# A message-passing layer on one core: layernorm by 625 nodes on 125 rows, with h's bfloat16 terms taken from it

## The chip, the core and the metric

The kernel runs on one core of a Trainium2 chip. A core has five engines that work side by side, each through its own queue of instructions in program order: TensorE (PE in the profile, its weight loads PEld), VectorE (DVE), ScalarE (ACT), GpSimd (POOL) and SyncE (SP). They wait for each other by semaphores. Transfers between the chip's memory and the on-chip memory (128 partitions, called rows here) are issued by SP, ACT or POOL and carried out by 16 DMA engines. TensorE writes into PSUM, a small memory that VectorE and ScalarE read.

The metric is device time in microseconds (us) of the whole kernel, the median of several runs; lower is better.

## The reference: what is computed

There are 6250 nodes of 64 features and 206250 edges, sorted by their destination. `x` is normalised and clipped, one message is formed for each edge from its source's row and the edge's own features, messages are summed by destination, and two small products with a residual end it:

```python
h = jnp.maximum(_layernorm(x, axis=-1), 0.0)
msg = jax.nn.relu(h[src] + edge_attr)
agg = jax.ops.segment_sum(msg, dst, num_segments=x.shape[0])
z = h + agg
out = x + jax.nn.relu(z @ W1 + b1) @ W2 + b2
```

## The kernel before

**Groups.** Edges go in 201 groups of 1024 (8 columns of 128 edges) and a short last one, numbered 0 to 201. For each group `load` (L171) brings the edge features `ea` by SP and the sources' rows `xg`, one column at a time, by an indirect transfer on POOL (`gather`, L161). The buffers of `ea` and `xg` are nine deep (`LOOK`); group g + 9 is loaded into group g's buffer once `messages(g)` (L465) has read it. `messages` adds the two and clips the sum, `one_hot` (L442) marks each edge's destination inside a window of 48 nodes, `window_sum` (L478) multiplies the two on TensorE, and `sum_into_z` (L438) adds the window to `z`, which holds h with its features on the rows.

**The first four groups** are gathered from `x` while h isn't yet there, and `norm_edges` (L420) normalises their rows on the spot. All later ones are gathered from `h_rows`, a copy of h in the chip's memory.

**Sets.** From group 4 on, two groups make a set of 16 columns, and six of them (four of an even group, two of an odd one) don't go by POOL: TensorE picks those rows from h on the chip. The nodes lie in ten parts of 625 (`SB`), each of five blocks of 125 (`BB`, `BN`). `hp` holds h as three bfloat16 terms that add up to it, a node to a row. For each set k, these stages run one or two sets ahead of their use: `hold` and `mask` (L335, L342) put an edge's place within its part and its node's number into one-hot form; `source` (L351) multiplies them into a list of wanted nodes, which makes a trip through the chip's memory to be spread over all rows (`source_row`, `sources`); `find` (L370) compares that list with the node numbers of each row; `slots_of` (L386) multiplies the result with `hp`; `back` (L378) compares `spots`, which each edge's place was written to earlier, with place numbers; and `pick` (L411) multiplies to bring each edge its row. The order of all this is written out by hand in `half` (L532), with no scheduler behind it.

**The beginning.** `x_sb` holds x with four nodes to a row in blocks of 512 nodes, twelve blocks and a rest of 106. `ln_head` (L187: mean, subtraction, squares) and `ln_rows` (L199: variance, root, h) run over three blocks at a time, then over the rest; `ln_rows` also writes `h_rows`, and `ln_turn` (L217) transposes h into `z`. Between these, `ranks` (L249), a generator with a `yield` after each of its steps, works out each set edge's part, its node inside the part, and its place; four of its steps run beside the layernorm, eight inside `norm_edges` of groups 0 to 3. ScalarE's queue starts with ten loads (L101 to L122): the rest of `src`, all of `dst`, the tails of both, and the four weights. After the layernorm `slot` is made from `dst` (L598 to L612). Groups 0 to 3 then run (L616). After them, `h_rows` is read back with 125 nodes to a row's block and split into the three terms (L626 to L636), edges' spots are worked out, transposed and written (L637 to L648), the first set's stages run alone (L651 to L655), and the main loop begins.

**The end.** `hidden`, `result` and `store` (L488 to L516) finish blocks of 512 nodes as soon as all edges of a block are summed, one stage at a time through `blocks_behind` (L520); `hidden` also loads the block's old rows `xb`. The last lines do so for block 11 and for the rest of 106 nodes.

The lines of the main order:

```python
        for g in range(2 * K0):
            half(g, sets=False)
        for _ in steps:
            pass
    ln_stack.close()
...
    spot(K0)
    hold(K0)
    mask(K0)
    for g in range(2 * K0):
        half(g, groups=False)
    for g in range(2 * K0, NG + 1):
        half(g)
```

Of the kernel before, what the change touches and what calls it, by code (L numbers as in the profile page):

```python
# [20 lines left out]
P = 128  # L21
# [6 lines left out]
TJ = 3  # L28
# [9 lines left out]
XC = 3  # L38
# [23 lines left out]
def kernel(  # L62
# [29 lines left out]
    x_sb = lnp.tile([P, NB + 1, R, D], F32, name="x_sb", bufs=1)  # L92
    for c in range(0, NB, XC):
        nc.sync.dma_start(
            out=x_sb[:, c:c + XC].rearrange("p b r d -> p b (r d)"),
            in_=x[c * P * R:(c + XC) * P * R, :].rearrange("(b p r) d -> p b (r d)", p=P, r=R),
        )
    nc.sync.dma_start(out=x_sb[:TN, NB, 0, :], in_=x[NB * P * R:, :])


    nc.scalar.dma_start(out=src_sb[:, RAW * G:C], in_=src_main[:, RAW * G:])  # L101
    nc.scalar.dma_start(out=dst_sb[:, :C], in_=dst_main)
# [7 lines left out]
    for t_sb, tail in ((src_sb, src_tail), (dst_sb, dst_tail)):  # L110
        flat = tail.rearrange("p j -> (p j)")
        nc.scalar.dma_start(out=t_sb[:, CP - CT:CP - 1], in_=flat[:TJ * P].rearrange("(p j) -> p j", j=TJ))
        nc.scalar.dma_start(out=t_sb[:, CP - 1:], in_=flat[TE - P:].rearrange("(p j) -> p j", j=1))
# [5 lines left out]
    nc.scalar.dma_start(out=w1_sb, in_=w1)  # L119
    nc.scalar.dma_start(out=w2_sb, in_=w2)  # L120
    nc.scalar.dma_start(out=b1_sb, in_=b1.rearrange("(d o) -> d o", o=1))
    nc.scalar.dma_start(out=b2_sb, in_=b2.rearrange("(o d) -> o d", o=1).to_broadcast([P, D]))  # L122
# [21 lines left out]
    hp = const.tile([P, KB, 3, D], BF16, name="hp")  # L144
    nc.vector.memset(hp[:, KB - 1], 0.0)
# [41 lines left out]
    def ln_head(c):  # L187
        xv, p, n = ((x_sb[:, c:c + XC].rearrange("p b r d -> p (b r) d"), P, XC * R) if c < NB
                    else (x_sb[:TN, NB, 0:1, :], TN, 1))
        s = lnp.tile([P, XC * R], F32, name="ln_s")  # L190
        nc.vector.tensor_reduce(s[:p, :n], xv, AX.X, ALU.add)
        nc.vector.tensor_scalar_mul(s[:p, :n], s[:p, :n], 1.0 / D)
        xc = lnp.tile([P, XC * R, D], F32, name="ln_xc")
        nc.vector.tensor_tensor(xc[:p, :n], xv, s[:p, :n].unsqueeze(2).to_broadcast([p, n, D]), ALU.subtract)
        sq = lnp.tile([P, XC * R, D], F32, name="ln_sq")
        nc.scalar.activation(sq[:p, :n], xc[:p, :n], AF.Square)
        return c, xc, sq, p, n

    def ln_rows(c, xc, sq, p, n):  # L199
        v = lnp.tile([P, XC * R], F32, name="ln_v")  # L200
        nc.vector.tensor_reduce(v[:p, :n], sq[:p, :n], AX.X, ALU.add)
        nc.scalar.activation(v[:p, :n], v[:p, :n], AF.Sqrt, bias=eps_sb[:p], scale=1.0 / D)
        nc.vector.reciprocal(v[:p, :n], v[:p, :n])
        h = lnp.tile([P, XC * R, D], F32, name="ln_h", bufs=3)
        nc.vector.scalar_tensor_tensor(h[:p, :n], xc[:p, :n], 0.0,
                                       v[:p, :n].unsqueeze(2).to_broadcast([p, n, D]),
                                       op0=ALU.max, op1=ALU.mult)
        if c < NB:
            nc.sync.dma_start(
                out=h_rows[c * P * R:(c + XC) * P * R, :].rearrange("(b p r) d -> p b (r d)", p=P, r=R),  # L210
                in_=h.rearrange("p (b r) d -> p b (r d)", r=R),
            )
        else:
            nc.sync.dma_start(out=h_rows[NB * P * R:, :], in_=h[:TN, 0, :])
        return c, h

    def ln_turn(c, h):  # L217
        for b in range(XC if c < NB else 1):
            pt = psum.tile([D, R, P], F32, name="rows", bufs=2)
            n0 = (c + b) * P * R  # L220
            if c < NB:
                for r in range(R):
                    nc.tensor.transpose(pt[:, r, :], h[:, b * R + r, :], ident)
                nc.scalar.copy(z[:, n0:n0 + P * R].rearrange("d (p r) -> d r p", r=R), pt)
            else:
                nc.tensor.transpose(pt[:, 0, :TN], h[:TN, 0, :], ident[:TN, :TN])
                nc.scalar.copy(z[:, n0:N], pt[:, 0, :TN])
# [5 lines left out]
    nc.gpsimd.iota(nodes_of, pattern=[[P, BB]], base=1, channel_multiplier=1, allow_small_or_imprecise_dtypes=True)  # L233
# [4 lines left out]
    fits = const.tile([P, KS, T], F32, name="fits")  # L238
# [10 lines left out]
    def ranks(pool):  # L249
# [11 lines left out]
        block = pool.tile([P, KS, T], F32, name="block")  # L261
        whole(block, src_f, BN)
        nc.vector.scalar_tensor_tensor(src_f, block, float(P - BN), src_f, op0=ALU.mult, op1=ALU.add)
# [20 lines left out]
        nc.vector.scalar_tensor_tensor(place, pt, float(-P), where, op0=ALU.mult, op1=ALU.add)  # L284
        nc.vector.tensor_scalar(fits, place, float(P), None, op0=ALU.is_lt)
        nc.vector.scalar_tensor_tensor(place, place, 1.0, fits, op0=ALU.add, op1=ALU.mult)

# [98 lines left out]
    def slots_of(k, m, n):  # L386

        ps = psum.tile([P, 2, 3 * D], F32, name="rows", bufs=2)
        for i in range(n):
            for b in range(BB):  # L390
                nc.tensor.matmul(ps[:, i], found[k][:BN, b, m + i, :],  # L391
                                 hp[:BN, (m + i) * BB + b].rearrange("p t d -> p (t d)"),
                                 start=(b == 0), stop=(b == BB - 1))
# [25 lines left out]

    def norm_edges(xg):  # L420
# [6 lines left out]
        next(steps, None)  # L427
# [3 lines left out]
        next(steps, None)  # L431
# [55 lines left out]

    def hidden(c):  # L488
# [4 lines left out]
        xb = work.tile([P, R, D], F32, name="xb")  # L493
        nc.sync.dma_start(out=xb[:p, :r].rearrange("p r d -> p (r d)"),
                          in_=x[n0:n0 + p * r, :].rearrange("(p r) d -> p (r d)", r=r))
# [36 lines left out]
    def half(g, groups=True, sets=True):  # L532
# [4 lines left out]
        if groups:  # L537
            enter(g + AHEAD)
# [9 lines left out]
        if groups:  # L548
            if g >= LAG:
                sum_into_z(g - LAG)  # L550
                blocks_behind(g - LAG)
            messages(g)
        if now and not even:
            slots_of(k + 1, 8, 2)
        if groups:
            take(g + 1)
# [5 lines left out]
        if groups and g >= 1:  # L562
            window_sum(g - 1)
# [15 lines left out]
        if groups:  # L579
            one_hot(g)  # L580
# [4 lines left out]
    with tc.tile_pool(name="rank", bufs=1) as rank:  # L585
        steps = ranks(rank)
        for c in range(0, NB + 1, XC):
            heads.append(ln_head(c))
# [7 lines left out]
        ln_turn(*rows[-1])  # L596

# [18 lines left out]
        for g in range(2 * K0):  # L616
            half(g, sets=False)
        for _ in steps:
            pass
    ln_stack.close()  # L620
    nc.vector.tensor_tensor(of_sets(slot, True), of_sets(slot, True), fits[:, :, :EVEN], ALU.mult)
    nc.vector.tensor_tensor(of_sets(slot, False), of_sets(slot, False), fits[:, :, EVEN:], ALU.mult)

    with tc.tile_pool(name="nodes", bufs=2) as nodes:

        for k, n in ((0, KB // 2), (KB // 2, KB - 1 - KB // 2), (KB - 1, 1)):  # L626
            p = min(BN, N - k * BN)
            h = nodes.tile([P, KB // 2, D], F32, name="h_nodes")
            if p == BN:
                nc.sync.dma_start(out=h[:BN, :n], in_=h_rows[k * BN:(k + n) * BN, :].rearrange("(k p) d -> p k d", p=BN))  # L630
            else:
                nc.sync.dma_start(out=h[:p, 0, :], in_=h_rows[k * BN:, :])
            nc.scalar.copy(hp[:p, k:k + n, 0, :], h[:p, :n])
            nc.vector.tensor_tensor(h[:p, :n], h[:p, :n], hp[:p, k:k + n, 0, :], ALU.subtract)
            nc.scalar.copy(hp[:p, k:k + n, 1, :], h[:p, :n])
            nc.vector.tensor_tensor(hp[:p, k:k + n, 2, :], h[:p, :n], hp[:p, k:k + n, 1, :], ALU.subtract)  # L636
        spot_f = nodes.tile([P, KS, T], F32, name="spot_f", bufs=1)  # L637
        nc.vector.scalar_tensor_tensor(spot_f, part, float(P), place, op0=ALU.mult, op1=ALU.add)
        spot_i = nodes.tile([P, KS * T], I16, name="spot_i", bufs=1)
        nc.vector.scalar_tensor_tensor(spot_i, spot_f.rearrange("p k t -> p (k t)"), float(BIAS - 1),  # L640
                                       fits.rearrange("p k t -> p (k t)"), op0=ALU.add, op1=ALU.mult)
        for c in range(0, KS * T, P):
            n = min(P, KS * T - c)
            turned = psum.tile([P, P], BF16, name="rows", bufs=2)
            nc.tensor.transpose(turned[:n], spot_i[:, c:c + n].bitcast(BF16), ident_b)
            sp = nodes.tile([P, P], BF16, name="sp")
            nc.scalar.copy(sp[:n], turned[:n])
            nc.sync.dma_start(out=spot_rows[c:c + n, :], in_=sp[:n])  # L648
    hot = ctx.enter_context(tc.tile_pool(name="hot", bufs=2))

    spot(K0)  # L651
    hold(K0)
    mask(K0)
    for g in range(2 * K0):
        half(g, groups=False)  # L655
# [83 lines left out]
```

## Time and profile before

| what | value |
|---|---|
| median of 3 runs | 1381.69 us (1381.45 to 1382.79) |
| the profiled execution | 1382.11 us, of it 1380.3 us in the span |
| busy, share of the span | PE 1251.2 (91%), PEld 1172.7 (85%), DVE 1194.2 (87%), ACT 510.0 (37%), POOL 1016.6 (74%) |
| chain that ended last | PE 50%, POOL 15%, DMA 12%, DVE 10%, issue 10%, ACT 2% |
| first gather from h_rows, last one | 51.96 us, 1362.37 us |
| last output transfer issued | 1375.91 us |

How to read it: the profile is one execution, from whose records the time of each instruction is known. A line of the costliest groups or of the timeline gives engine, source line, operation, output and inputs, shape, and in brackets how long the engine had stood before it and what ended that. "issue" stands for a wait that nothing in the records explains. DMA-issuing instructions are shown with a q (SPq, ACTq). A share of busy time is a mean over stages with different limits, so what holds the end has to be read stage by stage.

### The profile page before, as it was taken

The page shows a single profiled execution, that of the slowest core. Times are in us where ns is not written, and L with a number is a line of the kernel's source. Part 1 is how long each engine was busy: PE and PEld are TensorE (multiplying, and loading weights), DVE is VectorE, ACT ScalarE, POOL GpSimd, SP SyncE. Part 2 cuts the span into 40 slices and gives each one's busy share as a digit, 9 for nine tenths or more (in the row PEclk, how much of TensorE's full clock was granted, in tenths as well). Part 3 has the DMA queues.
Part 4 walks back from the last instruction along what each step waited for, and adds up shares of the span by engine and source line. Part 5 has one row for each costly group of instructions (what it writes and reads, how often), then busy time and mean ns, then how long its engine had stood idle before and what let it go on. Part 6 is the DMA issues. An engine that isn't in the chain of part 4 may idle for free.

```text
span 1380.3 us, 37812 instructions
## 1 busy us (share of the span) xinstructions
PE 1251.2 (91%) x15010; PEld 1172.7 (85%) x15010; DVE 1194.2 (87%) x2872; ACT 510.0 (37%) x1365; POOL 1016.6 (74%) x1029
## 2 busy tenths in 40 slices
PE   1623899999999999999999999999999999999997
PEld 0413799999999999999999998999998998988996
DVE  6765989889899899899899899899899898888984
ACT  2321334333433334334344333443334333433432
POOL 7671767777777777777777777777777777777773
PEclk9766999999999999999999999999999999999999
DMA  5332434444444444444444444444444344443431
GB/s 169 92 71 55 117 85 120 108 106 118 124 105 113 117 119 123 112 109 115 120 118 123 103 115 115 123 112 100 122 118 123 105 117 111 123 102 108 121 88 26
DMA packets 107888, 150.78 MB, mean 109 GB/s; under 512 B 33817, under 2 KB 52761, under 8 KB 107705
## 3 DMA queue, kind: packets, MB, share of 16 engines
q1 hardware_dynamic: 73881, 113.18, 28.2%
q0 software_dynamic: 32576, 33.42, 12.6%
q8 instruction: 119, 1.95, 0.6%
q10 hardware_dynamic: 1248, 1.70, 0.4%
q14 instruction: 64, 0.52, 0.1%
HBM read 144.60 MB, written 3.61 MB: 107 GB/s over the span
## 4 chain that ended last, share of the span: by engine, by line
PE 50%; POOL 15%; DMA 12%; DVE 10%; issue 10%; ACT 2%; DVEq 0%; SPq 0%; ACTq 0%; POOLq 0%
PE pick L417 23%; PE rows L391 16%; POOL xg L163 15%; PE agg L484 8%; DMA xg<-h_rows,src_sb 6%; DVE backs L383 3%; DMA ea<-in_edge_attr_dram 2%; DVE full L472 2%; PE rows L356 2%; DMA sources<-source_row 2%; DVE found L375 1%; DMA source_row<-source 1%; PE rows L505 1%; ACT picked L399 1%; DVE full L470 1%
## 5 line engine op out<-in xcount | busy, mean ns | idle before, releaser
L163 POOL DMA_INDIRECT xg<-h_rows,src_sb x986 | 982.1, 996 | 334.1 <-issue 258.6
L417 PE MATMUL pick<-picked,backs 128*128 128x192 bf16 x5940 | 524.0, 246 | 22.2 <-ACT pick L408 19.5
L417 PEld LDWEIGHTS <-backs 128*128 128x128 bf16 x5940 | 495.3, 98 | 26.7 <-issue 20.1
L391 PE MATMUL rows<-hp,found 125*128 125x192 bf16 x4950 | 465.2, 248 | 7.0 <-DVE found L375 6.1
L391 PEld LDWEIGHTS <-found 125*128 125x128 bf16 x4950 | 409.5, 98 | 18.7 <-DVE found L375 7.8
L383 DVE TENSOR_SCALAR backs<-spots,ids 128x768 bf16<-128x768 int16 x990 | 339.5, 415 | 0.0
L399 ACT CAST picked<-rows 128x384 bf16<-128x384 f32 x495 | 236.3, 477 | 277.4 <-PE rows L391 273.3
L375 DVE TENSOR_SCALAR found<-sources,nodes_of 125x1280 bf16<-125x1280 int16 x495 | 251.3, 572 | 36.7 <-DMA sources<-source_row 36.2
L472 DVE TENSOR_REDUCE full<-pick 128x128 f32<-128x512 f32 x297 | 207.7, 699 | 72.0 <-PE pick L417 41.4
L484 PEld LDWEIGHTS agg<-oh,msg 128*64 128x64 f32 x3224 | 205.0, 139 | 32.9 <-issue 17.9
L484 PE MATMUL agg<-oh,msg 128*64 128x48 f32 x3224 | 230.2, 225 | 0.6 <-ACT msg L475 0.6
L358 ACT CAST source<-rows 10x128 int16<-10x128 f32 x99 | 25.2, 254 | 464.2 <-PE rows L356 459.5
L475 ACT ACTIVATE msg<-full 128x512 f32<-128x512 f32 x202 | 119.5, 591 | 33.2 <-DVE full L472 20.3
L470 DVE TENSOR_TENSOR full<-full,xg 128x256 f32<-128x256 f32 (+1 forms) x202 | 98.7, 489 | 19.8 <-DMA xg<-h_rows,src_sb 15.4
L446 DVE TENSOR_TENSOR oh<-slot,wslots 128x384 f32<-128x384 int16 x202 | 109.6, 542 | 0.0
L338 DVE TENSOR_TENSOR holds<-place,wslots 128x768 f16<-128x768 f32 x99 | 93.2, 941 | 6.2 <-DMA spot_rows<-sp 6.2
L462 ACT COPY full<-ea 128x256 f32<-128x256 f32 (+1 forms) x202 | 87.0, 431 | 0.0
L408 ACT COPY pick<-ea 128x128 f32<-128x128 f32 x297 | 72.8, 275 | 0.0
L356 PE MATMUL rows<-holds,mask 128*10 128x128 f16 x594 | 50.1, 221 | 4.8 <-DVE mask L348 4.8
L356 PEld LDWEIGHTS <-mask 128*10 128x10 f16 x594 | 31.8, 88 | 22.1 <-issue 20.2
L440 DVE TENSOR_TENSOR z<-z,agg 64x48 f32 x202 | 38.3, 189 | 5.6 <-issue 2.9
L163 POOL DMA_INDIRECT xg<-in_x_dram,src_sb x32 | 32.7, 1021 | 11.2 <-issue 9.4
(105 smaller groups left out, 282.3 us busy)
## 6 DMA issues: line engine op xcount, KB each, us to landing
ea<-in_edge_attr_dram SPq DMA_DIRECT2D x201, 256.0 KB
sources<-source_row SPq DMA_DIRECT2D x99, 320.0 KB
spots<-spot_rows SPq DMA_DIRECT2D x99, 192.0 KB
xg<-h_rows,src_sb POOLq DMA_INDIRECT x986
source_row<-source SPq DMA_DIRECT2D x99, 2.5 KB
x_sb<-in_x_dram SPq DMA_DIRECT2D x4, 384.0 KB
h_rows<-ln_h SPq DMA_DIRECT2D x4, 384.0 KB
xb<-in_x_dram SPq DMA_DIRECT2D x12, 128.0 KB
```

Source lines behind the costliest of these rows:

```text
L163: nc.gpsimd.indirect_dma_start(out=xg[:, j, :], out_offset=None, in_=rows[:, :], in_offset=bass.IndirectOffsetOnAxis(ap=idx[:, j:j + 1], a ...
L356: nc.tensor.matmul(ps, mk[:, t, :], oh[:, t, :], start=(t == 0), stop=(t == T - 1))
L375: nc.vector.tensor_scalar(found[k][:BN, b].rearrange("p m s -> p (m s)"), row[:BN], nodes_of[:BN, b:b + 1], None, op0=ALU.is_equal)
L383: nc.vector.tensor_scalar(backs[k][:, m].rearrange("p t s -> p (t s)"), row, ids[:, m:m + 1], None, op0=ALU.is_equal)
L391: nc.tensor.matmul(ps[:, i], found[k][:BN, b, m + i, :], hp[:BN, (m + i) * BB + b].rearrange("p t d -> p (t d)"), start=(b == 0), stop=(b ...
L399: nc.scalar.copy(picked[k][:, m:m + n], halves.pop((k, m)))
L417: nc.tensor.matmul(pk[:, u, :3].rearrange("p t d -> p (t d)"), backs[k][:, m, t0 + i + u, :], picked[k][:, m], start=(m == 0), stop=(m == ...
L446: nc.vector.tensor_tensor(oh[:, lo:], slot[:, cols_of(g)].unsqueeze(2).to_broadcast([P, n, W]), wslots[:, :W].unsqueeze(1).to_broadcast([P ...
L470: nc.vector.tensor_tensor(full[:, lo:m], full[:, lo:m], xg[:, lo:m], ALU.add)
L472: nc.vector.tensor_reduce(full[:, m + i:m + i + c], pk[:, :c].rearrange("p j t d -> p j d t"), AX.X, ALU.add)
L475: nc.scalar.activation(msg[:, lo:], full[:, lo:], AF.Relu)
L484: nc.tensor.matmul(pa, msg[:, j, :], oh[:, j, :], start=(j == lo), stop=(j == G - 1))
```

## The change

- Layernorm runs over five pairs of parts, 625 nodes each, with 125 rows in use and five consecutive nodes to a row (`x_sb`, `ln_head`, `ln_rows`, `ln_turn`). There is no rest block. All five h tiles are kept.
- `hp` has 125 rows, and its three terms are made from those h tiles by `ln_parts`, a generator whose steps run in `norm_edges` of the first groups, around the steps of `ranks` (`fill`, `split_step`). The reload of `h_rows` and the pool `nodes` are gone. A node's number inside its part is now its row times five plus its place (`nodes_of`), so `ranks` needs no block number.
- On ScalarE's queue the load of `dst` comes after the second square, its tails and the weights after the last transposed copies.
- The spots are worked out, transposed and written, and `slot` is cleared where an edge is in a set, in the last step of `ranks`, inside group 3.
- `half` loses its `groups` argument; the first set's stages stand in a list of their own, with the sources of sets 2 and 3 both sent before the first `find`, and the z sums of groups 0 and 1 between.
- At the end the rows of x for the last nodes are loaded ahead, block 11's product comes before the last window sum, and its store before the last z sums.

```diff
-XC = 3
+XC = 2
-    x_sb = lnp.tile([P, NB + 1, R, D], F32, name="x_sb", bufs=1)
+    x_sb = lnp.tile([BN, SB, BB, D], F32, name="x_sb", bufs=1)
+    for m in range(0, SB, XC):
+            out=x_sb[:, m:m + XC].rearrange("p m b d -> p m (b d)"),
+            in_=x[m * PART:(m + XC) * PART, :].rearrange("(m p b) d -> p m (b d)", p=BN, b=BB),
...
-    nc.scalar.dma_start(out=dst_sb[:, :C], in_=dst_main)
-    for t_sb, tail in ((src_sb, src_tail), (dst_sb, dst_tail)):
+    for t_sb, tail in ((src_sb, src_tail),):
-    nc.scalar.dma_start(out=w1_sb, in_=w1)
...
+    def ln_turn(m, h):
+        for i in range(XC):
+            zv = z[:, (m + i) * PART:(m + i + 1) * PART].rearrange("d (p b) -> d b p", b=BB)
+            for b, n in ((0, 3), (3, 2)):
+                pt = psum.tile([D, 3, BN], F32, name="rows", bufs=2)
+                for r in range(n):
+                    nc.tensor.transpose(pt[:, r, :], h[:, i * BB + b + r, :], ident[:BN, :BN])
+                nc.scalar.copy(zv[:, b:b + n], pt[:, :n])
+
+    def ln_parts(m, h):
+        hv = hp[:, m * BB:(m + XC) * BB]
+        rest = lnp.tile([BN, XC * BB, D], F32, name="ln_xc", bufs=3)
+        nc.scalar.copy(hv[:, :, 0], h)
+        yield
+        nc.vector.tensor_tensor(rest, h, hv[:, :, 0], ALU.subtract)
+        nc.scalar.copy(hv[:, :, 1], rest)
+        yield
+        nc.vector.tensor_tensor(hv[:, :, 2], rest, hv[:, :, 1], ALU.subtract)
...
-    nc.gpsimd.iota(nodes_of, pattern=[[P, BB]], base=1, channel_multiplier=1, allow_small_or_imprecise_dtypes=True)
+    nc.gpsimd.iota(nodes_of, pattern=[[1, BB]], base=1, channel_multiplier=BB, allow_small_or_imprecise_dtypes=True)
...
-        block = pool.tile([P, KS, T], F32, name="block")
-        whole(block, src_f, BN)
-        nc.vector.scalar_tensor_tensor(src_f, block, float(P - BN), src_f, op0=ALU.mult, op1=ALU.add)
...
+        fits = pool.tile([P, KS, T], F32, name="fits")
+        spot_f = pool.tile([P, KS, T], F32, name="src_f")
+        nc.vector.scalar_tensor_tensor(spot_f, pt, float(P), place, op0=ALU.mult, op1=ALU.add)
+        for c in range(0, KS * T, P):
+            nc.tensor.transpose(turned[:n], spot_i[:, c:c + n].bitcast(BF16), ident_b)
+            sp = work.tile([P, P], BF16, name="sp")
+            nc.scalar.copy(sp[:n], turned[:n])
+            nc.sync.dma_start(out=spot_rows[c:c + n, :], in_=sp[:n])
+        nc.vector.tensor_tensor(of_sets(slot, True), of_sets(slot, True), fits[:, :, :EVEN], ALU.mult)
+        nc.vector.tensor_tensor(of_sets(slot, False), of_sets(slot, False), fits[:, :, EVEN:], ALU.mult)
...
+    def fill():
+        split_step()
+        next(steps, None)
+        split_step()
+
+    def split_step():
+        while split:
+            if next(split[0], True) is None:
+                break
+            split.pop(0)
...
-        next(steps, None)
+        fill()
...
-            if g >= LAG:
-                sum_into_z(g - LAG)
+        if g >= LAG and sets:
+            sum_into_z(g - LAG)
...
-        for c in range(0, NB + 1, XC):
-            heads.append(ln_head(c))
+        for m in range(0, SB, XC):
+            heads.append(ln_head(m))
+            if len(heads) == 2:
+                nc.scalar.dma_start(out=dst_sb[:, :C], in_=dst_main)
...
+        split = [ln_parts(*r) for r in rows]
+        for t_sb, tail in ((dst_sb, dst_tail),):
+            nc.scalar.dma_start(out=t_sb[:, CP - CT:CP - 1], in_=flat[:TJ * P].rearrange("(p j) -> p j", j=TJ))
+        nc.scalar.dma_start(out=w1_sb, in_=w1)
...
-        for k, n in ((0, KB // 2), (KB // 2, KB - 1 - KB // 2), (KB - 1, 1)):
-                nc.sync.dma_start(out=h[:BN, :n], in_=h_rows[k * BN:(k + n) * BN, :].rearrange("(k p) d -> p k d", p=BN))
-            nc.scalar.copy(hp[:p, k:k + n, 0, :], h[:p, :n])
-            nc.vector.tensor_tensor(h[:p, :n], h[:p, :n], hp[:p, k:k + n, 0, :], ALU.subtract)
...
-    for g in range(2 * K0):
-        half(g, groups=False)
+    for k in (K0, K0 + 1):
+        hold(k)
+        mask(k)
+        source(k)
+        spot(k)
+    for g in range(2 * K0 - LAG):
+        sum_into_z(g)
+    find(K0)
+    back(K0)
+    for m in range(0, SB, 2):
+        slots_of(K0, m, 2)
+        slots_out(K0, m, 2)
+    room(2 * K0)
+    pick(2 * K0)
+    spot(K0 + 2)
+    hold(K0 + 2)
+    mask(K0 + 2)
+    find(K0 + 1)
     for g in range(2 * K0, NG + 1):
         half(g)
+    xbs[NB] = old_rows(NB)
+    for c in sorted(hid):
+        res[c] = result(c, *hid.pop(c))
     window_sum(NG)
+    for c in sorted(res):
+        store(c, *res.pop(c))
     for g in range(NG + 1 - LAG, NG + 1):
         sum_into_z(g)
-        blocks_behind(g)
-    blocks_behind(NG + 1)
-    blocks_behind(NG + 2)
     store(NB, *result(NB, *hidden(NB)))
```

## The prediction

> All times are us from the start of the profiled execution of before (span 1380.3; its own time 1382.11, 0.4 above the median of the runs, 1381.69).
>
> **What bounds the kernel now.** I read the costliest groups and POOL's waits first, since one line holds POOL for the whole span.
>
> ```profile
> L163 POOL DMA_INDIRECT xg<-h_rows,src_sb x986 | 982.1, 996 | 334.1 <-issue 258.6
> ```
> ```profile
> POOL xg L163 <- issue: 268.1, 864, 4.8
> POOL xg L163 <- DVE full L470: 32.3, 12, 26.3
> ```
>
> A gather costs 0.996 busy and, nearly always, 0.30 of issue gap: 1.30. The two other things here are one wait of 4.8 and one of 26.3. Then the busy time by stretch (columns: PE, PEld, DVE, ACT, POOL; instructions in brackets):
>
> ```profile
> 52.00:137.00 85.00, 31.33 (x237) 24.33 (x237) 54.13 (x110) 18.85 (x37) 46.28 (x44) 0.60 0.29 70
> ...
> 437.00:737.00 300.00, 298.09 (x3657) 282.20 (x3655) 276.83 (x666) 116.97 (x324) 229.68 (x231) 1.00 0.45 116
> ...
> 1237.00:1363.00 126.00, 119.41 (x1447) 113.37 (x1446) 105.15 (x256) 47.13 (x129) 96.43 (x98) 0.99 0.38 97
> ```
>
> In the middle PE is full (298.09 of 300) and eats the gathers that lie ready; near the end it is not (119.41 of 126), while POOL issues at one rate throughout. A set takes PE 148 instructions, 12.1 long in the middle, and POOL 10 gathers, 13.0. So POOL is the slower one, has 44 gathers in hand when the sets start, and is caught up late. **The end is POOL's: the time of its restart, plus the remaining 942 gathers at 1.30, plus the tail.** The timeline shows the restart and what leads to it:
>
> ```profile
> 15.73 1.58 ACT L196 ACTIVATE ln_sq<-ln_xc 128x768 f32<-128x768 f32 x2 [12.47 <-DMA w_sb<-in_w_dram]
> ...
> 51.96 0.95 POOL L163 DMA_INDIRECT xg<-h_rows,src_sb  x1 [4.80 <-issue]
> ...
> 81.04 18.43 SPq L630 DMA_DIRECT2D h_nodes<-h_rows  x3
> ...
> 110.44 0.94 POOL L163 DMA_INDIRECT xg<-h_rows,src_sb  x1 [0.30 <-issue]
> ...
> 116.31 0.95 DVE L338 TENSOR_TENSOR holds<-place,wslots 128x768 f16<-128x768 f32 x1 [6.17 <-DMA spot_rows<-sp]
> ...
> 124.06 2.40 DVE L375 TENSOR_SCALAR found<-sources,nodes_of 125x1280 bf16<-125x1280 int16 x5 [5.91 <-DMA sources<-source_row]
> ...
> 137.68 0.94 POOL L163 DMA_INDIRECT xg<-h_rows,src_sb  x1 [26.30 <-DVE full L470]
> ```
>
> POOL fills its nine buffers (groups 4 to 12: 44 gathers) by 111.4 and sits until messages(4) frees group 4's buffer. Before that lie the reload of h, its splitting (92.4 to 108.6), the spots' turn, and the first set. So the sum is made to 137.68, stage by stage.
>
> **Layernorm.** ScalarE issues ten loads before its first square, until 15.67. Seven of them (dst whole, dst's two tail loads, four weights) go behind it; three remain, so the square follows the first head. Five blocks of 640 elements per row replace four of 768 and one of 64. From the 768 and 512 rows (0.95 and 0.69) a 640 pass is 0.83 on VectorE; a head is 1.9, a block's rows 2.3 to 2.6.
>
> The new loads and stores have 125 rows. The one large 125-row transfer of before is the h_nodes reload:
>
> ```profile
> q1 hardware_dynamic: 2008, 0.51, 37.6%
> ```
>
> That is the DMA view for 93 to 99: 0.51 MB in 6 (85 GB/s), the queue's share near a third of the engines; a 128-row h_rows write held 375 to 387 GB/s. The Trainium skill (DMA: Bandwidth & Descriptors, "Why a DMA increments its semaphore by 16 and not by 1") speaks against the change: a transfer runs on the largest number up to 16 that divides its outer dimension; for 125, five engines. By rule a 320 KB block takes 320/(387 x 5/16 = 121 GB/s) = 2.6; by the row, whose pieces are 256 bytes against 1280 now, 3.9. I take 2.6 as an estimate. Before, src and dst (1.6 MB) held two thirds of the traffic until 8.4; with src alone x's blocks land at about 7.7, 10.3, 12.9, 15.5, 18. Only the second is waited for; at 3.9 it comes 2 later.
>
> VectorE then runs: heads to 12.2; first rows to 14.9 (before 19.15); step 1 (2.3) 17.1; head 19.0; rows 21.3; comparisons (3.9) 25.2; head and rows 29.4; step 3, without the three block passes (0.50, 0.70, 0.79), 1.0: 30.4; the fifth head, now full, 32.3; rows 34.6; step 4 (5.6) 40.2. The last root stands on ScalarE behind the third turn's z copies, now four of 375 or 250 columns (0.73 and 0.52 between the 512 and 106 rows: 2.5), to 42.9; last h at 44.0. Its write is issued there and lands in 0.75 + 2.6 + 0.6: **POOL starts at 48.1** against 51.96; its x gathers end at 47.2 anyway.
>
> **slot.** ScalarE now issues dst's tail after the remaining eight z copies (5.0), at 48.1; it lands about 2 later. VectorE idles from 44.0; base (0.5), its product (0.65) and slot (1.83 + 0.3) end at **53.6** against 54.6. The skill (same page, "Rules for kernel authors") says to issue a load early and wait late. Left early, this load would let slot end at 50.4: the move costs 3.2 here.
>
> **Groups 0 to 3.** VectorE is full there: 30.23 of 31.5. The three terms of h now come in ten pieces each for ScalarE and VectorE. Between the 1600 and 64 rows (1.83, 0.22) a VectorE piece of 640 is 0.82; ten are 8.2. ScalarE's ten casts of 0.72 lie beside (it was busy 6.59 of 31.5). I add 0.2 stall for each of three early groups. The register load ahead of the first z sum (2.9) leaves this stretch; spot_f and spot_i (1.55) enter it. Group 0: 7.7 + 2.5 + 0.2; 1: 7.8 + 3.3 + 0.2; 2: 7.7 + 2.5 + 0.2; 3 as far as spot_i: 7.5. Sum 39.6: spot_i stands at **93.2**, against 110.1. The reload and the wait for it, from 90.1 to 108.6, are gone.
>
> **First set.** Behind spot_i VectorE has 3.05 of work: the slot products (0.9), reciprocal, product, sum, one_hot. This hides the transposes of spots (2.8, by the sp copies that wait for their writes); without it the first hold would wait as at 116.31. hold and mask take 1.4; PE may be 0.35 late behind window_sum(2), ScalarE 0.3 behind five sp copies and the messages; then the trip by DRAM as before (118.91 to 124.06, 5.15): found at 93.2 + 11.2 = **104.4**. The register load, two z sums, second hold and mask (5.3) lie inside that trip; uncovered they would cost 2.
>
> Before, 12.9 went from found to the add that frees the buffer, with a 2.61 wait for the second sources. Now that source is sent ahead: found 2.4, back 3.4, hold 0.95, mask 0.43, found 2.4, z 0.2, add 0.42, release 0.3 = 10.5. **POOL restarts at 114.9**: 22.8 earlier. Its own 44 gathers from 48.1 end at 107, so VectorE still decides, by 8. PE starts its first picks at 112.8 (before 134.07): 21.3 earlier, but has slack at the end.
>
> **Tail.** The rows of x for the last block are asked for early:
>
> ```profile
> 1375.33 0.23 DVE L513 TENSOR_TENSOR xb<-xb,b_sb 106x64 f32<-106x64 f32 x1 [3.10 <-DMA xb<-in_x_dram]
> ```
>
> With them there, the next wait is the product of the last block, which goes 0.9 later, as block 11's result (1.05) and store (0.83) pass ahead. The last output leaves at 1373.9 rather than 1375.9: 2.0; at most 2.7 (the wait on the transfer), at least 1.
>
> Steady sets: half() issues the same instructions; a node's place inside its part changes, no shape does. Nothing.
>
> **Sum:** 22.8 + 2.0 = 24.8; 1382.11 - 24.8 = 1357.3; less 0.4 for the median, **1357**.
>
> **Rivals.**
> - Restart at POOL's own pace (0.09). If groups 0 to 3 take less than summed (ScalarE's slack is real, my stalls are guesses), POOL never stands: 107 rather than 114.9, and 2.0 to 2.7 in the tail: 1349. This is the cap: of the reload's time, POOL needed most for its own gathers.
> - The terms choke the groups (0.10). Each hangs on a ScalarE cast that queues with squares, roots and messages; a full round trip per piece (1.6 to 1.9 in before's splitting at L634 to L636) instead of 0.2 costs some 10: 1367. Against: 1.8 of `here` products lie between cast and use.
> - No gain (0.03). The restart moves and the end doesn't, were POOL waiting elsewhere: 1381. Against: no POOL wait after 137.68 exceeds 0.6.
> - Slower (0.08): 125-row transfers on one engine. 387/16 = 24 GB/s; x lands at 69, not 18, against 30.4 where the fifth head wants it: 39 lost, and the last write takes 13. POOL starts at 98, restarts at 157: 1382 + 19 - 2 = 1399. It decides from a landing at 55, 31 GB/s; the one such row in the trace shows 85.
>
> **Numbers.** The forecast has 0.70, with its own spread of 1350 to 1364 (slot 2 either way, stalls 0 to 5, tail 1 to 2.7). The range reaches to the cap below and into the choked case above: 1349 to 1366. A change under 0.2%, 2.8, can't be told from none. Faster 0.89, same 0.03, slower 0.08.
>
> **What would show it.** The first square near 9.6; POOL's first h_rows gather at 48; spot_i near 93; found at 104; POOL's one long wait about 8 and ending near 115; gathers at 1.30 after it; no wait for xb at the end. Wrong: a first head that waits for x past 12, VectorE idle in groups 0 to 3, a POOL wait over 1 in the sets.

## The result, and the profile after

The changed kernel takes **1370.20 us** (median of 4 runs, 1369.88 to 1370.91) beside 1382.24 for the kernel before (1381.45 to 1383.61): a ratio of 0.9908, 95% interval 0.9895 to 0.9921. It is faster, by 12.0 where the prediction said 25, and outside its range. The profiled execution took 1370.91, its span 1369.2.

POOL's waits after (columns: us in total, times, longest):

```profile
POOL xg L155 <- DMA ea<-in_edge_attr_dram: 8.3, 1, 8.3
POOL xg L155 <- DVE full L489: 18.6, 15, 7.9
```

POOL's long wait for a freed buffer fell from 26.3 to 7.9, as predicted; but all its waits for that add are 18.6: one of the 14 others is 5.54 (last line below) and two are 0.89; the remaining eleven are no longer than the usual gap of 0.30. The timeline after, the lines that answer to those of before:

```profile
9.36 0.82 DVE L183 TENSOR_REDUCE ln_s<-x_sb 125x10 f32<-125x640 f32 x1 [6.81 <-DMA x_sb<-in_x_dram]
12.14 0.82 DVE L183 TENSOR_REDUCE ln_s<-x_sb 125x10 f32<-125x640 f32 x1 [0.89 <-DMA x_sb<-in_x_dram]
14.21 0.74 ACT L188 ACTIVATE ln_sq<-ln_xc 125x640 f32<-125x640 f32 x1 [2.19 <-DVE ln_xc L186]
19.11 0.33 ACTq L613 DMA_DIRECT2D dst_sb<-in_dst_main_dram  x1
19.50 0.30 ACT L195 ACTIVATE ln_v<-ln_v,eps_sb 125x10 f32<-125x10 f32 x1 [4.55 <-DMA x_sb<-in_x_dram]
...
52.46 0.34 ACTq L625 DMA_DIRECT2D dst_sb<-in_dst_tail_dram  x1
55.93 0.96 POOL L155 DMA_INDIRECT xg<-h_rows,src_sb  x1 [8.35 <-DMA ea<-in_edge_attr_dram]
57.98 0.14 DVE L632 COPY dst_sb<-dst_sb 1x1 int32<-1x1 int32 x1 [9.50 <-DMA dst_sb<-in_dst_tail_dram]
...
100.36 0.78 DVE L283 SCALAR_TENSOR_TENSOR spot_i<-src_f,fits 128x594 int16<-128x594 f32 x1
112.72 2.57 DVE L382 TENSOR_SCALAR found<-sources,nodes_of 125x1280 bf16<-125x1280 int16 x5 [1.56 <-DMA sources<-source_row]
122.86 0.94 POOL L155 DMA_INDIRECT xg<-h_rows,src_sb  x1 [7.91 <-DVE full L489]
123.69 0.70 DVE L491 TENSOR_REDUCE full<-pick 128x128 f32<-128x512 f32 x1 [1.10 <-PE pick L424]
125.34 0.70 DVE L491 TENSOR_REDUCE full<-pick 128x128 f32<-128x512 f32 x1 [0.95 <-PE pick L424]
163.04 1.10 POOL L155 DMA_INDIRECT xg<-h_rows,src_sb  x1 [5.54 <-DVE full L489]
```

Read from the top. The first square starts at 11.29, both are done by 14.95, and ScalarE is free. But the next thing in its queue is the issue of `dst`'s load, which stands until 19.11, and the first root is queued behind it. In brackets the root's wait is put down to x; VectorE had been reading the second block since 12.14, and the issue just ahead of the root is the nearer reading. The last h leaves at 48.5 (the rest of `h_rows` goes out at 48.51). Then VectorE idles 9.50 for `dst`'s tail, which is issued at 52.46 and used at 57.98. From `slot`'s end (61.7) to POOL's restart the stages are as long as predicted. Just behind the restart VectorE stands 1.10 and 0.95 for TensorE's first picks, and at 163.04 POOL stands once more, 5.54. Before had a wait of the same gather too:

```profile
175.20 1.10 POOL L163 DMA_INDIRECT xg<-h_rows,src_sb  x1 [2.42 <-DVE full L470]
```

Against before, POOL's restart is 14.8 earlier (137.68 to 122.86), the gather behind the second stall 12.2 (175.20 to 163.04), the last gather 9.25 (1362.37 to 1353.12), the end of the span 11.1.

### The profile page after: what moved, and what is told of

It reads as the page before. It is cut to its first block, busy times and chain, and to the rows that moved or that the text cites. A ratio compares the mean times of both kernels' runs of the same rounds, so it can differ in the third digit from the quotient of the medians.

```text
span 1369.2 us, 37804 instructions
## 1 busy us (share of the span) xinstructions
PE 1256.3 (92%) x15011; PEld 1176.4 (86%) x15011; DVE 1190.9 (87%) x2872; ACT 510.8 (37%) x1376; POOL 1018.5 (74%) x1029
## 5 line engine op out<-in xcount | busy, mean ns | idle before, releaser
L155 POOL DMA_INDIRECT xg<-h_rows,src_sb x986 | 983.5, 997 | 323.0 <-issue 253.6
L212 PE MATMUL rows<-ident,ln_h 125*64 125x125 f32 x50 | 10.4, 347 | 34.0 <-DVE ln_h L198 21.1
```

What stands on the lines that cost most here:

```text
L155: nc.gpsimd.indirect_dma_start(out=xg[:, j, :], out_offset=None, in_=rows[:, :], in_offset=bass.IndirectOffsetOnAxis(ap=idx[:, j:j + 1], a ...
```

## The experiments

The first four kernels ran beside the kernel before at 1381.66, the last four at 1383.05. To set them against the changed kernel I take the difference of the ratios to before, times 1382; an interval of 0.0015 either way is 2 us, so these differences carry some 2 to 3. A single profile carries about as much: the restart of POOL, 137.68 in before, is at 136.69 in experiment 6 and at 135.57 in experiment 5, whose kernels are the same up to there.

### 1. dst's load leaves ScalarE's queue

```diff
     loaded = [load(g) for g in range(RAW)]
+    nc.sync.dma_start(out=dst_sb[:, :C], in_=dst_main)
...
-            if len(heads) == 2:
-                nc.scalar.dma_start(out=dst_sb[:, :C], in_=dst_main)
```

> The changed kernel with one line moved: the load of dst is issued by SP, behind the first four edge loads, and no longer by ScalarE between the second square and the first root. In the changed kernel that issue started at 19.11 us though ScalarE was free at 14.95, and the first root came at 19.50. Theory A (ScalarE's queue stands on the issue[...], and the first root stands behind it): first root near 15.2, last h at 44.5 instead of 48.5, slot's end near 58 instead of 61.7, POOL's restart near 119 instead of 122.9, time 1366.5 (3.5 less). Rival B (x itself arrives too late on its few engines): the first root moves, but the third and later heads then wait for x; last h no earlier than 47.5, time within 1 of 1370.

Measured: 1363.55 (1363.14 to 1364.75), ratio 0.9872 (0.9856 to 0.9889): 5.0 less than the changed kernel. The timeline of this run:

```profile
14.97 0.30 ACT L196 ACTIVATE ln_v<-ln_v,eps_sb 125x10 f32<-125x10 f32 x1
19.44 0.33 SPq L178 DMA_DIRECT2D dst_sb<-in_dst_main_dram  x1
52.77 0.14 DVE L631 COPY dst_sb<-dst_sb 1x1 int32<-1x1 int32 x1 [8.51 <-DMA dst_sb<-in_dst_tail_dram]
```

The issue is still held, now on SP, to nearly the same time (19.44 after 19.11); but the root no longer stands behind it and runs at 14.97, 4.5 earlier, with x arriving as before. So it was the issue that held ScalarE, not x. The last h (44.25), `slot` (56.6), found (107.23) and POOL's restart (117.25) follow by 4.3 to 5.6; 5.0 is more than the 3.5 expected, by less than such a difference carries.

### 2. dst's tails go first

```diff
-    for t_sb, tail in ((src_sb, src_tail),):
+    for t_sb, tail in ((src_sb, src_tail), (dst_sb, dst_tail)):
...
-        for t_sb, tail in ((dst_sb, dst_tail),):
-            flat = tail.rearrange("p j -> (p j)")
...
```

> The changed kernel with dst's two tail loads back at the head of ScalarE's queue, right behind src's tails; the four weights stay late. Theory A (VectorE's wait of 9.5 us, 48.5 to 58.0, is the late tail: issued at 52.46 behind the z copies, landed 5.5 later beside the edge loads): base made at 48.7, slot's end near 56 because its product on TensorE still stands behind the last transposes, restart near 117, time 1364.5 (5.7 less). Rival B (the two issues cost ScalarE their 1.2 to 5 us each[...], as in the kernel before, and push the first square from 11.3 to 15): last h 3 later, time 1368.

Measured: 1360.41 (1356.44 to 1362.53), ratio 0.9841 (0.9818 to 0.9864): 9.3 less than the changed kernel, more than expected. Its timeline:

```profile
9.44 0.34 ACTq L110 DMA_DIRECT2D dst_sb<-in_dst_tail_dram  x1
14.37 0.33 ACTq L613 DMA_DIRECT2D dst_sb<-in_dst_main_dram  x1
15.35 0.35 SPq L146 DMA_DIRECT2D ea<-in_edge_attr_dram  x1
19.58 0.80 SPq L146 DMA_DIRECT2D ea<-in_edge_attr_dram  x2
48.28 1.83 DVE L634 SCALAR_TENSOR_TENSOR slot<-dst_sb,rows 128x1608 int16<-128x1608 int32 x1 [4.33 <-PE rows L632]
```

The second tail was held too, to 9.44; the first square needed ScalarE only at 11.44, so this cost nothing. The surprise is that the main load then went at 14.37 and the root at 15.10: ScalarE no longer stands on that issue. The hold itself is not gone. It has moved to SP, whose four loads of edge features are spread from 12.2 to 20.4 (after: 10.7 to 15.3): the third of them goes only at 19.58, 3.9 behind the second. So the run shows two terms at once. They come apart by the time from the last h to `slot`'s end: 13.2 after (48.5 to 61.7), 12.4 in experiment 1 (44.25 to 56.6), 6.8 here (43.5 to 50.25). **The late tail costs about 6**, not 3.2. It is not all of that time: `slot` now waits 4.33 for its product on TensorE, which stands for a buffer, `rows`, until ScalarE's last transposed copy but one ends at 47.58.

### 3. 112 and 13 rows

```diff
-        nc.sync.dma_start(
-            out=x_sb[:, m:m + XC].rearrange("p m b d -> p m (b d)"),
-            in_=x[m * PART:(m + XC) * PART, :].rearrange("(m p b) d -> p m (b d)", p=BN, b=BB),
-        )
+        for lo, hi in ((0, 112), (112, BN)):
+            nc.sync.dma_start(
+                out=x_sb[lo:hi, m:m + XC].rearrange("p m b d -> p m (b d)"),
+                in_=x[...].rearrange("(m p b) d -> p m (b d)", p=BN, b=BB)[lo:hi],
+            )
```

The write of `h_rows` is cut in the same way.

> The changed kernel with each load of x and each write of h_rows cut into two transfers of 112 and 13 rows instead of one of 125. Theory A (125 rows run on five of 16 engines, 112 on 16 and 13 on 13; the changed profile has one write at 116 GB/s and 31.1% of the engines): first block of x at 6.5 instead of 9.36, no wait for the second, the issue of dst's load delayed by less than 1 instead of 4.2, last h near 43, last write landed by 47 so that POOL's first gather from h_rows is at 47.5 instead of 55.9, time 1363 (7 less). Rival B (the row count has nothing to do with the rate; pieces of 1280 bytes are as slow on any number of rows): all of this within 1 of the changed kernel, time 1370, or 1 more for ten more issues on SP.

Measured: 1359.49 (1356.26 to 1364.05), ratio 0.9851 (0.9829 to 0.9873): 7.9 less than the changed kernel. Its timeline:

```profile
7.26 0.82 DVE L184 TENSOR_REDUCE ln_s<-x_sb 125x10 f32<-125x640 f32 x1 [4.71 <-DMA x_sb<-in_x_dram]
9.07 0.81 DVE L184 TENSOR_REDUCE ln_s<-x_sb 125x10 f32<-125x640 f32 x1
10.98 0.35 ACTq L615 DMA_DIRECT2D dst_sb<-in_dst_main_dram  x1
11.71 0.30 ACT L196 ACTIVATE ln_v<-ln_v,eps_sb 125x10 f32<-125x10 f32 x1
47.33 0.14 DVE L634 COPY dst_sb<-dst_sb 1x1 int32<-1x1 int32 x1 [7.18 <-DMA dst_sb<-in_dst_tail_dram]
```

The first block is there 2.1 earlier, the second without a wait, and the load of `dst`, from the same place on ScalarE as after, isn't held at all: the root comes 7.8 earlier. The last h is done at 40.15 and POOL's first gather is at 47.65 (expected: 43 and 47.5). So shorter transfers ahead free this issue. How slow the uncut ones were is in the DMA view after, for 27 to 32, where the first two blocks of h are being written (queue, packets, MB, share of 16 engines):

```profile
q1 hardware_dynamic: 456, 0.58, 31.1%
```

0.58 MB in 5 us is 116 GB/s, at a share of 5/16 = 31.3%. The number of engines can be read from views that hold the write of one block of h alone: 35.2 to 40.2 after, and 27.3 to 32 in this run.

```profile
q1 hardware_dynamic: 255, 0.32, 22.1%
```
```profile
q1 hardware_dynamic: 279, 0.32, 24.3%
```

The 125 rows go in two pieces each, 250 packets. What is over, 5 packets after and 29 = 16 + 13 here, is 4 bytes long in the trace and as many as theory A has engines at work; a write of 128 rows in before (34.6 to 40) has 400 packets, 384 pieces and 16. From its first packet to its last, that write takes 3.8 after and 1.4 here; the five writes of h take 3.0 to 5.4 after and 1.4 to 2.6 here. And from 4 to 14 the engines stood half idle after, where before had them full (columns: PE, PEld, DVE, ACT, POOL, granted clock, DMA share, GB/s); the first row is of before:

```profile
4.00:14.00 10.00, 0.00 (x0) 0.00 (x0) 4.13 (x6) 0.00 (x0) 7.32 (x7) 1.00 1.02 365
```
```profile
4.00:14.00 10.00, 0.00 (x0) 0.00 (x0) 3.62 (x6) 0.74 (x1) 7.13 (x8) 1.00 0.46 132
```

### 4. find_left out of POOL's way

```diff
-        if g == 8:
+        if g == 100:
             find_left()
```

> The changed kernel with find_left (7.6 us on VectorE in one piece) called after group 100 instead of group 8; nothing else. Theory A (at group 8 POOL is as far ahead as its nine buffers allow, so any delay of messages stops it: 5.54 us at 163.0; at group 100 it is some groups behind that limit): no POOL wait over 1 us after the restart, last gather 5 earlier, time 1365. Rival B (TensorE loses the same 6 us wherever the piece stands, and the end follows TensorE): time within 1 of 1370.

Measured: 1364.90 (1364.18 to 1365.99), ratio 0.9879 (0.9863 to 0.9896): 4.0 less than the changed kernel. POOL's last waits over 1 in this run:

```profile
123.84 0.95 POOL L155 DMA_INDIRECT xg<-h_rows,src_sb  x1 [8.38 <-DVE full L489]
132.45 0.94 POOL L155 DMA_INDIRECT xg<-h_rows,src_sb  x1 [1.21 <-DVE full L489]
```

The 5.54 is gone; the 1.21 behind the restart, where after had 0.89, is a little over the expected 1. In experiments 1, 2, 3 and 7, which leave `find_left` where it was, the wait is 5.54 each time. `find_left` (L307 to L325 after) works out which edges fell outside their window; it holds VectorE in one piece of 7.8, from 154.10 to 161.87, just as POOL is nine buffers ahead and needs VectorE to free one.

### 5. The same edit on the kernel before

The edit of experiment 4, on before.

> The kernel before with find_left after group 100 in place of group 8. Theory A (what find_left costs is the time that POOL stands behind it, since POOL's lead is then at its greatest): the wait of 2.42 at 175.2 goes and with it about 2: 1379.5. Theory B (the work costs the same wherever it stands, and the gain of the same edit on the changed kernel came from elsewhere): as much as there, 5: 1376.5; or nothing, 1381.7.

Measured: 1380.86 (1377.28 to 1384.58, 12 runs), ratio 0.9982 (0.9971 to 0.9994): 2.5 less than before, for a wait of 2.42. POOL's waits on the add that frees a buffer, in total 32.3 before (the long one, 24.8 here after 26.3, lies ahead of the edit):

```profile
POOL xg L163 <- DVE full L470: 27.0, 8, 24.8
```

So, as far as differences of 2 to 3 can tell, the stretch costs what POOL waits behind it, in both kernels: 2.4 before and 5.5 after. The change made that wait 3.1 longer, or 1.9 beside the 3.67 that it takes in experiment 6, whose kernel is that of before up to there. The piece itself is no longer (7.6 before, 7.8 after), but VectorE comes to it 31.2 behind POOL's restart, 28.7 before. Most of these 2.5 are the two waits for TensorE's picks, 2.05 together, which before doesn't have: there the first picks start 2.9 ahead of the add that lets POOL go (134.07 and 136.99), after only 0.4 ahead (121.78 and 122.17). No run here takes these two waits away.

### 6. The tail alone

```diff
+    xbs[NB] = old_rows(NB)
+    for c in sorted(hid):
+        res[c] = result(c, *hid.pop(c))
     window_sum(NG)
+    for c in sorted(res):
+        store(c, *res.pop(c))
     for g in range(NG + 1 - LAG, NG + 1):
         sum_into_z(g)
-        blocks_behind(g)
-    blocks_behind(NG + 1)
-    blocks_behind(NG + 2)
```

This is the change's end, on the kernel before.

> The kernel before with the change's end alone: the last old rows of x asked for early, block 11's product ahead of the last window sum, its store ahead of the last sums. Theory A (the prediction's tail): the wait of 3.10 for the old rows is gone and 2.0 of it is kept: 1379.6. Theory B (the last transfer or the last sums set the end anyway): 1381.7, no change.

Measured: 1382.73 (1379.98 to 1384.28, 12 runs) beside 1383.05, ratio 0.9995 (0.9984 to 1.0005). Time alone settles nothing: the interval holds no change and, barely, the predicted 2. The timelines show the last output's add, before and in this run:

```profile
1375.66 0.23 DVE L514 TENSOR_TENSOR o<-o,xb 106x64 f32<-106x64 f32 x1
```
```profile
1373.48 0.22 DVE L522 TENSOR_TENSOR o<-o,xb 106x64 f32<-106x64 f32 x1 [1.49 <-ACT o L515]
```

With its last gather at 1362.32 (before: 1362.37), the add comes 11.16 behind it where before had 13.29 (1375.66): 2.1 less. From the last gather to the span's end it is 16.5 after 17.9: 1.4 less. The step does what was said in the profile; that it moves the median by 2 isn't shown.

### 7. The terms of h in one stretch

```diff
     def fill():
-        split_step()
         next(steps, None)
-        split_step()
```

All pieces then run behind group 3.

> The changed kernel with h's three terms made in one stretch behind group 3, not in pieces inside groups 0 to 3. Theory A (the pieces cost what the prediction gave them): groups 0 to 3 take some 9 less, the five blocks behind them some 14, so found and POOL's restart come 5 later and the end with them: 1375. Theory B (each piece inside the groups waits a full trip between ScalarE and VectorE, the prediction's rival of choked groups): groups 0 to 3 take 15 or more less, and the kernel isn't slower than 1370.

Measured: 1376.25 (1372.40 to 1379.00), ratio 0.9951 (0.9935 to 0.9968): 5.9 more than the changed kernel. The timeline of this run, spot_i and the first piece:

```profile
91.46 0.78 DVE L283 SCALAR_TENSOR_TENSOR spot_i<-src_f,fits 128x594 int16<-128x594 f32 x1
100.44 0.82 DVE L220 TENSOR_TENSOR ln_xc<-ln_h,hp 125x640 f32<-125x640 f32 x1 [5.42 <-ACT hp L218]
```

spot_i comes at 91.46 rather than 100.36, 8.9 earlier; group 0 starts 0.7 earlier in this run (61.26, after 61.98), so inside groups 0 to 3 the ten pieces cost 8.2, against a summed 8.8 (8.2 of work and three stalls of 0.2). The rival of choked groups is out. In one stretch VectorE waits 0.79 for a cast of ScalarE in each of the five blocks, the first find comes at 120.00, 7.3 later, and the end about 6.

### 8. Four edits together

Experiments 1, 2, 3 and 4 in one kernel.

> The changed kernel with four edits at once: the load of dst issued by SP behind the first four loads of edge features, dst's tails at the head of ScalarE's queue, x and h_rows moved in pieces of 112 and 13 rows, find_left after group 100. Theory A (the three lost terms are the whole of what is missing, and POOL's gathers set the end): first block of x near 7.3, last h near 40, slot near 44, spot_i near 83, found near 95; VectorE would let POOL go at 105, but POOL's own 44 gathers from 47.5 last until 106.7, so it hardly stands: no wait of POOL on a freed buffer over 2 anywhere. POOL's stream then starts 4.5 earlier and loses the waits of 26.3 and 2.4: 33 earlier, and 2 at the tail, less some 3 of longer gathers: 1350, within 1347 to 1353. Theory B (the next bound is another engine): not below 1356, what the single edits gave, with several waits of POOL over 1 spread over the sets.

Measured: **1352.25** (1351.92 to 1355.33), ratio 0.9775 (0.9760 to 0.9791), the fastest kernel here: 18.4 less than the changed one, 31 less than before. Its timeline:

```profile
46.19 1.83 DVE L635 SCALAR_TENSOR_TENSOR slot<-dst_sb,rows 128x1608 int16<-128x1608 int32 x1 [4.72 <-PE rows L633]
109.01 0.94 POOL L156 DMA_INDIRECT xg<-h_rows,src_sb  x1 [2.42 <-DVE full L492]
117.64 0.94 POOL L156 DMA_INDIRECT xg<-h_rows,src_sb  x1 [1.22 <-DVE full L492]
```

The time lies inside theory A's 1347 to 1353, and far under B's 1356. POOL gathers from 47.47 and stands 2.42 and 1.22 before it runs on. A's wording "no wait over 2" is missed by 0.4: the last h is done at 41.0, `slot` waits 4.72 for its product, as in experiment 2, and ends at 48.2, not at 44, and found starts at 98.75, not at 95. The four single gains (5.0, 9.3, 7.9, 4.0) add up to 26, the four together bring 18.4. The first three overlap, since each of them frees ScalarE of the same held issue; how much of the 8 that explains was not measured. VectorE still decides the restart here, 2.42 behind POOL's own gathers.

## Why the prediction was wrong in size

**What held.** POOL's restart sets the end, and VectorE decides it. From the last gather to the end of the span it is 16 to 18 in all ten profiles, and behind the restart POOL has no wait above 1.6 in any of them but the one at find_left. That the long wait is 7.91, predicted 8, is luck in part: VectorE was 8.0 late, and POOL's own gathers began 7.8 late (55.93, not 48.1). Both share the late last h (4.5); that the rest was alike, 3.5 and 3.3, is chance. Groups 0 to 3 as far as spot_i took 39.1 (summed: 39.6), spot_i to found 11.7 (11.2), found to restart 10.1 (10.5). The pieces of h cost 8.2 (8.8 with stalls). The tail kept 1.85 of its 2.0 in the profile after (16.1 from the last gather to the span's end, 17.9 before). The traffic of 125-row transfers had a share of 5/16, and the second block of x came 2.78 behind the first: the prediction had an estimate of 2.6, from the rule of the Trainium skill (DMA: Bandwidth & Descriptors, "Why a DMA increments its semaphore by 16 and not by 1") that 125 rows run on five engines, and 3.9 by the row. The rule has the engines right, as the packets in experiment 3 show, and gives the better price for these loads; the writes of h took 3.0 to 5.4.

**The step that failed first: Layernorm.** The prediction put x's blocks at 7.7, 10.3, 12.9, 15.5 and 18, said "Only the second is waited for", and left the last h at 44.0. The start of x was 1.7 late (9.36), its second block 1.8 (12.14). But the larger part is elsewhere: the sum counted the load of `dst` among seven loads that "go behind" the first square, as a thing gained, and then gave its issue no time in its new place. It was held 4.2 on ScalarE, with root, h and everything after them behind it: the first block's h was done at 20.9, not 14.9 (1.8 + 4.2), the last at 48.5. Experiment 1 takes the issue out of that queue, with x as late as after, and has the last h at 44.25, where 44.0 was summed. That this comes out is luck: its first h is 1.5 late (16.4), and the rest, summed as 29.1, took 27.9. The lateness of x passes on to the end of the layernorm: with x early and nothing held, experiment 3 has its first h at 13.1 and its last at 40.15, 4.1 ahead of experiment 1. The prediction priced five engines per block of x; what it left out was that an issue behind such transfers is held and keeps the engine that gives it. The write of the last h took longer as well: POOL's first gather came 7.4 behind its issue (48.51 to 55.93), summed as 4.0. This cost nothing, since VectorE decides the restart later still.

**The second: slot.** "It lands about 2 later", by short loads on a quiet queue. It took 5.5 (52.46 to 57.98), 4.9 in experiment 1 and 3.6 in experiment 3, beside six loads of edge features that SP issues from 48.81 on. Why it took longer than 2 was not tried. With both steps `slot` ended at 61.7, not 53.6: 8.1 of the 13.6 that are missing in the profile (24.8 summed, 11.1 or 11.2 found). The skill's rule to issue early and wait late (same page, "Rules for kernel authors") spoke against this move; the prediction priced the move at 3.2, and experiment 2 puts it at about 6.

**The third: find_left.** The sum went from the restart to the end at POOL's pace, and against the rival of no gain it said "no POOL wait after 137.68 exceeds 0.6". That was misread: before's trace has 2.42 at 175.20 and 0.89 at 188.80, and the total of 32.3 in the shown line leaves 6 beside the 26.3. The sum gave this wait nothing, before or after. After, it is 5.54; the lead of the restart falls from 14.8 to 12.2 there. Experiments 4 and 5 show a cost of that order, 4.0 and 2.5. The sum also let TensorE's first picks start at 112.8, 21.3 earlier than before, and gave VectorE no wait for them; they start at 121.78, and VectorE's 2.05 of waiting for them lie ahead of find_left.

**What is left:** 2.9 between that point and the last gather, where POOL has no wait over 1; see the last section. As a sum: 14.8 - 2.7 - 2.9 + 1.9 = 11.1.

**The rivals.** The cap, 1349 with no waiting, was not passed: the kernel of all four edits has 1352.25. Choked groups are refuted, and so are 125 rows on a single engine. The outcome was a case the prediction had no name for: the forecast's own mechanism, with 8 us lost ahead of the restart and some 5.6 behind it.

## What to carry to other kernels

An issue of a transfer is an instruction of the engine that gives it: when it is moved, ask which transfers will lie ahead of it then, and what computation stands behind it; put it on an engine whose next work is far off. Before a startup is built on a transfer, look at what its number of rows divides by: 125 rows ran on five engines here, and cut into 112 and 13 the same bytes were written in 1.4 us, not 3.8. And once a stall is shortened, look in the trace of before for every later wait of the same engine, however small: here one of 2.42 became 5.54.

## What the runs showed that was not expected

- The held issue moves. The same load of `dst` was issued at 19.11 (after), 19.44 (by SP), 14.37 (tails first) and 10.98 (112 and 13 rows). But in each of the first three some large load goes out only at 19.1 to 19.6, some 3.8 to 3.9 behind the issue before it: `dst` on ScalarE (SP's last edge load before it ends at 15.34), `dst` on SP, and with the tails first an edge load on SP. So the order of the issues decides which engine stands, not whether one does. Slow transfers are not needed for a hold: in before, with x on 128 rows, ScalarE stood from 4.85 to 9.48 between the two tail loads of `src`. Which limit holds an issue, no record shows. This stays open.
- The gathers' pace isn't one number. From the gather behind the second stall to the last one, where POOL has no wait over 1, it took 1187.2 in before (175.20 to 1362.37), 1190.1 in after, 1187.2 in experiment 1, 1189.3 in experiment 2 and 1184.9 in experiment 3; from the same gather on, 1193.5 in the kernel with four edits. In the same order, all 986 gathers were busy 982.1, 983.5, 980.4, 984.1, 979.2 and 987.2. Some 4 either way is thus beyond any sum of stages, and the 2.9 lost in after's profile lies within it: 2.8 of it are longer gathers (909.2, before 906.4), while the gaps between them are the same (276.0 and 276.2). What makes single gathers longer was not tried.
